# Moving the add of two expert results from VectorE to GpSimd at the end of a two-layer perceiver kernel

## The chip, the core and the metric

The kernel runs on one core of one Trainium2 chip. The metric is the device time of one execution in microseconds (us). Before the change the median of three runs is 888.03 us (887.79 to 888.46).

## What is computed

The reference runs two layers over `x`, 64 sequences of 32 rows of 256 values, 2048 rows in all, in float32. Only the last of six blocks matters here, a mixture of experts with two chosen experts per row and one shared expert:

```python
router_probs = softmax(flat @ router_w + router_b)
topk_probs, topk_idx = top_k(router_probs, 2)
weights = zeros_like(router_probs).at[arange(T)[:, None], topk_idx].add(topk_probs)
shared_out = gelu(flat @ sw1 + sb1) @ sw2 + sb2
h1 = gelu(einsum('td,edh->teh', flat, rw1) + rb1)
expert_out = einsum('teh,ehd->ted', h1, rw2) + rb2
mixed = einsum('ted,te->td', expert_out, weights)
x = x + shared_out + mixed
```

So each row of the output is x, plus the shared expert's row, plus two expert rows, each times its own weight.

## The kernel before

The 2048 rows are 4 groups (`NG`) of 4 tiles (`NT`) of 128 rows. `xs[g]` holds group g in SBUF as 128 partitions x 4 tiles x 256 values. The tiles of rows that go to experts are gathered, multiplied and written to a buffer in HBM, `r_rows`, by indirect DMAs that GpSimd issues (`outputs`, from L1948, issue at L1964). `r_rows` has one row for each pair of a row of x and one of its two choices.

When the last of these writes has landed, the end of the kernel begins, L2015 to L2064, and this is where the change is:

- **Loads** (L2020 to L2022). For each group and each choice (`which` is 0 or 1) SyncE issues one DMA of 512 KB from `r_rows` into `r[g][which]`, which has the shape of `xs[g]`: eight loads, in the order (0,0), (0,1), (1,0) and so on to (3,1).
- **Weights on ScalarE** (`weigh`, L2033). ScalarE multiplies tiles of `r` by the rows' weights, in place, one activation for each tile of 128x256. `by_scalar` (L2028) says which: in groups 0, 1 and 2 the tiles 2 and 3 of choice 0 and all four of choice 1; in group 3 all four of choice 0 and none of choice 1.
- **Sums on VectorE** (`sum_up`, L2039). For each choice and each pair of tiles: where ScalarE has weighted them, one `tensor_tensor` of 128x512 adds the pair to x; where not, two `scalar_tensor_tensor` of 128x256 multiply by the weight and add to x. So group 0, 1 or 2 takes two fused instructions (choice 0, tiles 0 and 1), then three adds of a pair (choice 0, tiles 2 and 3; choice 1, tiles 0 and 1; choice 1, tiles 2 and 3). Group 3 takes two adds and four fused instructions. Behind each pair of choice 1, SyncE issues a DMA of 256 KB from x to the output (L2053), eight in all.
- **Shared expert.** `fill_outputs` puts four matmuls for each tile on TensorE, into PSUM, and `settle` lets VectorE add the two tiles of such a bank to x (`x<-ps_so,x`, 128x512). Four of these pairs are left for the end. The first is settled ahead of `sum_up(0)`, the others one by one between the groups (L2058 to L2064). They use two banks in turn.

Every engine takes its instructions in the order in which the program names them (the switch at L511 keeps that order). So VectorE's order at the end is: settle, group 0, settle, group 1, settle, group 2, settle, group 3. ScalarE's order is the tiles of group 0, choice 0 before choice 1, then group 1 and so on. GpSimd has nothing to do after its last indirect write. Nothing that one engine does waits for another except where they touch the same part of a tile; such waits are semaphores that the framework puts in. The helper at L107 records nearly every operation, so in the profile lines are told apart by tiles: `x<-r,w,x` is the fused instruction, `x<-x,r` the add of a pair, `x<-ps_so,x` the settle, `r<-r,w` ScalarE's weighting.

Of the kernel before, what the change touches and what calls it, by code (L numbers as in the profile page):

```python
# [12 lines left out]
ALU = mybir.AluOpType  # L13
# [7 lines left out]
NG, NT = 4, 4  # L21
# [44 lines left out]
def perceiver_kernel(ctx: ExitStack, tc: tile.TileContext, a: dict, out: bass.AP):  # L66
# [32 lines left out]
    class InOrder:  # L99
# [12 lines left out]
    vector, scalar, gpsimd, sync = (  # L112
        InOrder(e) for e in (nc.vector, nc.scalar, nc.gpsimd, nc.sync)
    )
# [974 lines left out]
    def settle(n=None):  # L1089
        for _ in range(len(owed) if n is None else n):  # L1090
            owed.pop(0)()
# [529 lines left out]
    def mixture():  # L1621
# [395 lines left out]
        r = [(whole[:, 0], whole[:, 1]), (whole[:, 2], whole[:, 3])]  # L2017
# [6 lines left out]
        def weight(g, which, t):  # L2024
            at = which * nt + g * NT + t
            return pw[:, at : at + 1]

        def by_scalar(g, which):  # L2028
            if g == NG - 1 and which == 1:
                return ()  # L2030
            return range(NT) if which or g == NG - 1 else range(2, NT)

        def weigh(g):  # L2033
            for which in range(2):
                for t in by_scalar(g, which):
                    rows_t = r[g][which][:, t, :]
                    scalar.activation(rows_t, rows_t, AF.Copy, scale=weight(g, which, t))

        def sum_up(g):  # L2039
            for which in range(2):  # L2040
                for t0 in range(0, NT, 2):
                    if t0 in by_scalar(g, which):
                        x = xs[g][:, t0 : t0 + 2, :]
                        vector.tensor_tensor(x, x, r[g][which][:, t0 : t0 + 2, :], ALU.add)
                    else:
                        for t in range(t0, t0 + 2):
                            x = xs[g][:, t, :]
                            vector.scalar_tensor_tensor(
                                x, r[g][which][:, t, :], weight(g, which, t), x, ALU.mult, ALU.add
                            )  # L2050
                    if which == 1:
                        sync.dma_start(
                            out=out_view[g][:, t0 : t0 + 2], in_=xs[g][:, t0 : t0 + 2]  # L2053
                        )

        for g in range(NG):
            weigh(g)
        fill_outputs(2)  # L2058
        settle()
        sum_up(0)  # L2060
        for g in range(1, NG):
            fill_outputs(2)
            settle()
            sum_up(g)  # L2064

    out_view = out.rearrange("(g t p) d -> g p t d", g=NG, p=P)
    mixture()
    attention.close()

# [151 lines left out]
```

## Time and profile before

| what | value |
|---|---|
| median of three runs | 888.03 us |
| the profiled execution, its own time | 888.15 us |
| its span, first to last instruction | 886.4 us |
| granted TensorE clock, mean of the span | 0.992 |
| TensorE busy | 851.0 us (96%) |
| VectorE busy | 576.1 us (65%) |
| ScalarE busy | 438.5 us (49%) |
| GpSimd busy | 513.9 us (58%) |

The shares are means over the whole program. The part that the change touches is the last 21 us of the span, from 865.4 us on, when TensorE has only the shared expert left. In the views, DVE is VectorE, ACT is ScalarE, POOL is GpSimd, PE is TensorE and SP is SyncE; an operation is written out<-in by the names of tiles. A row of the timeline has the start and the length in us, merges neighbours of one kind (`x3` is three instructions), and shows in brackets the idle time ahead of it and who ended it. Two instructions of one engine overlap a little in the records, so the spacing of their starts is shorter than one's length.

### The profile page before, as it was taken

To read this page: it belongs to the slowest core of one execution; us is meant where nothing else is said; L and a number is where in the kernel's file an instruction comes from. 1 tells how busy PE (TensorE), PEld (TensorE's weight loads), DVE (VectorE), ACT (ScalarE), POOL (GpSimd) and SP (SyncE) were. 2 spreads that over 40 slices of the span, in tenths; PEclk is the share of its full clock that TensorE was granted. 3 is DMA by queue.
4 is the path that set the end of the run, shared out by engine and by line. 5 is a ranking of instruction groups with operands and counts; after the bars stand their busy time and mean duration, and the time that the engine had idled before them with its cause. 6 is when DMAs were issued, how large, how long until landed. Compare 5 with 4: busy or idle time off the path is not lost. (4 is left out here: it accounts for less than half of the span.)

```text
span 886.4 us, 22890 instructions
## 1 busy us (share of the span) xinstructions
PE 851.0 (96%) x8729; PEld 586.9 (66%) x8729; DVE 576.1 (65%) x1692; ACT 438.5 (49%) x1135; POOL 513.9 (58%) x1004
## 2 busy tenths in 40 slices
PE   7989999999999999999999999999999999999995
PEld 3566666665466666666666665666667568888894
DVE  6888777896777576885778756866766861111116
ACT  2756667674654555565445645575652323222224
POOL 4677777785774657575575754685651254555430
PEclk9999999999999999999999999999999999999999
DMA  6564433553110111110111101120010046777768
GB/s 216 146 164 119 120 92 96 143 138 104 54 55 24 34 54 55 55 55 2 55 54 56 55 1 55 55 73 25 3 36 2 24 169 219 232 232 232 220 191 290
DMA packets 66926, 88.77 MB, mean 100 GB/s; under 512 B 32480, under 2 KB 50688, under 8 KB 64768
## 3 DMA queue, kind: packets, MB, share of 16 engines
q1 hardware_dynamic: 62592, 76.95, 28.9%
q0 software_dynamic: 3456, 9.44, 3.2%
q8 instruction: 69, 1.13, 0.5%
q10 hardware_dynamic: 768, 0.92, 0.4%
q14 instruction: 41, 0.34, 0.1%
HBM read 65.78 MB, written 13.11 MB: 89 GB/s over the span
## 5 line engine op out<-in xcount | busy, mean ns | idle before, releaser
L107 ACT ACTIVATE e<-e,xnm 128x257 f32<-128x257 f32 x256 | 127.2, 499 | 43.7 <-DVE xnm L107 40.4
L119 PE MATMUL ps_k<-ct,w_w_l1x 128*128 128x512 f32 x256 | 122.8, 602 | 1.1 <-ACT yT L107 0.5
L107 POOL TENSOR_SCALAR e<-e,xsm 128x256 f32<-128x256 f32 x256 | 123.4, 500 | 0.0
L107 DVE CUSTOM_DVE_ANT_0 e<-ps_s,mask 128x257 f32<-128x257 f32 x256 | 93.5, 421 | 43.3 <-PE ps_s L119 43.1
L119 PE MATMUL ps_v<-w_w_l1x,ct 128*128 128x256 f32 x512 | 121.1, 379 | 0.0
L122 PE MATMUL ps_t<-cst,e 128*128 128x128 f32 x640 | 101.7, 281 | 2.3 <-DVE eT L107 2.0
L119 PEld LDWEIGHTS ps_v<-w_w_l1x,ct 128*128 128x128 f32 x512 | 93.4, 190 | 10.8 <-ACT y L107 0.2
L107 DVE COPY eT<-ps_t 128x512 f32<-128x512 f32 x124 | 85.1, 686 | 23.4 <-PE ps_t L122 23.3
L107 ACT ACTIVATE kT<-ps_k,vec 128x512 f32<-128x512 f32 x64 | 44.0, 687 | 97.9 <-PE ps_k L119 96.4
L107 POOL TENSOR_TENSOR x<-x,rows 128x256 f32<-128x256 f32 x96 | 70.0, 747 | 28.2 <-DVE y L107 24.9
L107 ACT ACTIVATE hTr<-ps_h,w 128x256 f32<-128x256 f32 (+1 forms) x80 | 31.4, 450 | 110.3 <-issue 89.4
L122 PEld LDWEIGHTS ps_t<-cst,e 128*128 128x128 f32 x640 | 71.4, 140 | 20.1 <-DVE eT L107 4.8
L107 DVE TENSOR_TENSOR og<-ps_o,b 128x512 f32<-128x512 f32 (+1 forms) x20 | 12.8, 638 | 105.6 <-PE ps_o L119 105.6
L119 PEld LDWEIGHTS ps_k<-ct,w_w_l1x 128*128 128x128 f32 x256 | 44.6, 190 | 42.0 <-issue 34.1
L1964 POOL DMA_INDIRECT r_rows<-og,lv x36 | 35.5, 986 | 60.8 <-DVE og L107 55.9
L119 PE MATMUL ps_h<-ygT,w 128*128 128x256 f32 (+1 forms) x320 | 67.2, 364 | 0.0
L107 ACT COPY v<-ps_v 128x512 f32<-128x512 f32 x80 | 46.4, 581 | 41.1 <-PE ps_v L119 40.7
L107 POOL TENSOR_TENSOR last<-e,xsm 128x4 f32<-128x4 f32 x64 | 15.3, 238 | 88.6 <-DVE xsm L107 87.1
L119 PE MATMUL ps_o<-w,hTr 128*128 128x256 f32 x288 | 65.3, 379 | 0.0
L119 PEld LDWEIGHTS ps_h<-ygT,w 128*128 128x128 f32 x320 | 56.0, 194 | 6.4 <-issue 0.2
L119 PEld LDWEIGHTS ps_o<-w,hTr 128*128 128x128 f32 x288 | 54.4, 190 | 7.2
L107 ACT ACTIVATE kb<-kT,cst 128x256 f32<-128x256 f32 x96 | 45.4, 512 | 23.8 <-POOL kT L107 23.7
(225 smaller groups left out, 1671.4 us busy)
## 6 DMA issues: line engine op xcount, KB each, us to landing
ct<-in_ctxT SPq DMA_DIRECT2D x16, 1024.0 KB
w<-in_ew SPq DMA_DIRECT2D x20, 514.0 KB
w<-in_ew SPq DMA_DIRECT2D x20, 512.0 KB
far<-part SPq DMA_DIRECT2D x126, 64.0 KB
v_rows<-v SPq DMA_DIRECT2D x16, 256.0 KB
vb<-v_rows SPq DMA_DIRECT2D x64, 64.0 KB
r<-r_rows SPq DMA_DIRECT2D x8, 512.0 KB
b<-in_eb SPq DMA_DIRECT2D x20, 128.0 KB
```

The source lines that it names most:

```text
L107: ins = getattr(self.engine, name)(*args, **kw)
L119: return kept(nc.tensor.matmul(ps, **args))
L122: return kept(nc.tensor.transpose(ps, src, eye))
L1964: wrote = nc.gpsimd.indirect_dma_start(out=r_rows, out_offset=bass.IndirectOffsetOnAxis(ap=write_i[:, at : at + 1], axis=0), in_=o[:, i, : ...
```

## The change

For groups 0, 1 and 2, GpSimd adds the weighted tiles 2 and 3 of choice 0 to the weighted tiles 2 and 3 of choice 1, in place in `r[g][1]`, with one `tensor_tensor` of 128x512. VectorE no longer adds that pair of choice 0 to x; the pair of choice 1, which now holds the sum of both, is added as before. Group 3 is as it was. In GpSimd's order the three adds come after all its indirect writes.

```diff
+        def added(g):
+            pair = r[g][0][:, 2:NT, :]
+            if g < NG - 1:
+                gpsimd.tensor_tensor(r[g][1][:, 2:NT, :], r[g][1][:, 2:NT, :], pair, ALU.add)
+
         def weigh(g):
...
         def sum_up(g):
             for which in range(2):
                 for t0 in range(0, NT, 2):
+                    if which == 0 and t0 == 2 and g < NG - 1:
+                        continue
                     if t0 in by_scalar(g, which):
...
         for g in range(NG):
             weigh(g)
+            added(g)
         fill_outputs(2)
```

## The prediction

> **What bounds the end now.** I read first the chain of work that ended last, in order of time:
>
> ```profile
> 877.56 1.06 DVE x L107 x3
> ...
> 879.08 1.34 DVE x L107 x3
> 880.42 0.09 issue
> ...
> 880.88 1.08 DVE x L107 x2
> ...
> 882.36 0.79 DVE x L107 x2
> ```
>
> It is VectorE alone, up to its last add into x. Then the timeline, VectorE alone and ScalarE alone:
>
> ```profile
> 871.88 1.49 DVE L107 TENSOR_TENSOR x<-x,r 128x512 f32<-128x512 f32 x2 [0.82 <-ACT r L107]
> 873.29 0.68 DVE L107 TENSOR_TENSOR x<-ps_so,x 128x512 f32<-128x512 f32 x1
> ...
> 877.88 1.89 DVE L107 TENSOR_TENSOR x<-x,r 128x512 f32<-128x512 f32 x3
> 879.68 0.68 DVE L107 TENSOR_TENSOR x<-ps_so,x 128x512 f32<-128x512 f32 x1
> 880.28 1.28 DVE L107 TENSOR_TENSOR x<-x,r 128x512 f32<-128x512 f32 x2
> 881.49 1.67 DVE L107 SCALAR_TENSOR_TENSOR x<-r,w,x 128x256 f32<-128x256 f32 x4
> ```
>
> ```profile
> 870.95 2.50 ACT L107 ACTIVATE r<-r,w 128x256 f32<-128x256 f32 x6 [0.60 <-DMA r<-r_rows]
> 873.89 2.51 ACT L107 ACTIVATE r<-r,w 128x256 f32<-128x256 f32 x6 [0.44 <-DMA r<-r_rows]
> 876.70 3.38 ACT L107 ACTIVATE r<-r,w 128x256 f32<-128x256 f32 x8 [0.30 <-DMA r<-r_rows]
> ```
>
> From 871.88 on VectorE shows no more idle time in brackets, to 883.15. ScalarE is paced by the loads; single rows of a narrower window give the ends of its tiles of groups 0, 1 and 2: 872.65, 875.60 and 878.41. VectorE runs close behind. It starts the last add of group 2 at 879.08, only 0.67 us after ScalarE's end. That margin decides this change. The loads' semaphores show the rest of the DMA side: (3,1) lands at 879.78, then six 256 KB outputs that had queued behind the loads land about 0.66 us apart (880.42 to 883.72), and the last two at 884.55 and 885.32, each about 2.15 us after its issue (882.39, 883.18).
>
> **What the change removes.** Three VectorE adds `x<-x,r` of 128x512. One lasts 0.684 us, but starts follow 0.60 us apart, so 3 x 0.60 = 1.8 us. Only about 0.26 us of it could reach the end: eight outputs at 0.66 us behind the last load give 879.78 + 8 x 0.66 = 885.06, against 885.32 now.
>
> **What it adds.** Three GpSimd adds of two SBUF inputs, 128x512. The row of groups has this form for another tile:
>
> ```profile
> L107 POOL TENSOR_TENSOR kT<-near,far 128x512 f32<-128x512 f32 x16 | 20.3, 1272 | 15.7 <-DMA far<-part 11.1 <-ACT kb L107 2.2 <-ACT yT L107 2.0
> ```
>
> I take 1.27 us (all 61 of this form: 1.262 least, 1.504 most). `near<-near,cst` starts 0.08 us after the ScalarE instruction it waited for; VectorE starts 0.035 us after GpSimd. So a new wait stands ahead of VectorE's last add of each group, and behind it in VectorE's queue stand the settle and the whole next group; SyncE's outputs wait for those. Without any disturbance the result of group g is there 0.08 + 1.27 + 0.035 = 1.39 us after ScalarE's end, but VectorE came 0.67 us after that end in group 2.
>
> **Shared reading.** A second cost appears where both engines read two SBUF inputs at once. The timeline at 190 us:
>
> ```profile
> 190.39 1.50 POOL L107 TENSOR_TENSOR qT<-near,far 128x512 f32<-128x512 f32 x1 [0.37 <-DMA far<-part]
> ...
> 191.21 1.23 DVE L107 TENSOR_TENSOR y<-y,big 128x512 f32<-128x512 f32 x1
> ...
> 191.86 1.18 POOL L107 TENSOR_TENSOR x<-x,rows 128x256 f32<-128x256 f32 x1
> ...
> 192.48 1.10 DVE L107 TENSOR_TENSOR q<-y,big 128x512 bf16<-128x512 f32 x1
> ```
>
> VectorE's add of two SBUF inputs takes 1.23 us instead of some 0.66 and ends 0.55 us after GpSimd's end (191.89); GpSimd's next takes 1.18 instead of 0.73 and ends 0.60 after VectorE's. They go by turns, and the one that waits ends about 0.13 us less than its own length after the other. The fused form suffers too: `conv<-yT,vec,conv` 128x248 takes 0.477 us alone and up to 0.83 beside GpSimd. An add with one input in PSUM doesn't: `x<-ps_p,x` takes 0.36 to 0.42 us with GpSimd beside it and without. So the settles stay free, while `x<-r,w,x` and `x<-x,r` queue with GpSimd.
>
> [...] With no 0.13 us back at each hand-over the sum below would be 2.26 us instead of 1.94; the rows above decide for the smaller.
>
> **The sum**, by starts in us of the profiled execution (spacing 0.60 for a pair, 0.39 for a fused one):
>
> - Group 0: GpSimd 872.65 + 0.08 = 872.73 to 874.00. VectorE ends its add of tiles 0 and 1 at 872.58, as before, then stands until 874.04. Settle 874.64. TensorE's last pair waits for that bank: it now starts some 1.3 us later than 874.03 and ends near 879.1, still ahead of its settle.
> - Group 1: fused 875.24 and 875.64. GpSimd asks at 875.68, behind the second fused one (ends 876.12): done 876.12 + 1.27 - 0.13 = 877.26. The add of tiles 0 and 1, asked for at 876.03, ends 877.26 + 0.55 = 877.81; the last add starts 877.73, settle 878.33.
> - Group 2: GpSimd 878.41 + 0.08 = 878.49 to 879.76. The first fused one, asked for at 878.93, ends 879.76 + 0.48 - 0.13 = 880.11; the next starts 880.03, the add of tiles 0 and 1 880.42, the last add 881.02.
>
> Before, that last one started at 879.08: **+1.94 us**. All behind it (settle, two adds, four fused, the last output, the closing) is the same queue at the same spacing, its loads long landed, and the last two outputs find the DMA queue empty, so it moves as a whole: span 886.40 + 1.94 = 888.34, own time 888.15 + 1.94 = 890.09. The profiled run stands 0.12 above the median, so 888.03 + 1.94 = 889.97; I say **890.0 us**.
>
> **Unknown: GpSimd's first arithmetic after indirect DMAs.** The trace has none. The nearest row is the turn the other way: the first indirect DMA after arithmetic started 0.84 us after its wait was over, later ones 0.28, and took 1.28 instead of 0.98, so (0.84 - 0.28) + 0.30 = 0.86 us extra. The low end is 0: nothing in GpSimd's row suggests a gain. With 0.86, group 0 ends at 874.86; GpSimd's second add then gets in first, and the same steps give a last add at 881.29, +2.2 us. I take 0, since the 9 us of idle time before may hide it, and keep +2.2 for the range. With all three adds as long as the longest row (1.50) as well, the steps give 881.75, +2.7, and the runs shown stand up to 0.43 above their median: 891.2 at the top.
>
> **Rivals.**
> 1. *No contention on these tiles.* Then only the new wait counts: the last add of group 2 starts at 878.49 + 1.27 + 0.035 = 879.80, **+0.71**, 888.7 us. For it: `near<-near,cst` on GpSimd keeps 1.27 us beside VectorE. Against: the rows at 190 us have exactly two SBUF inputs on each side.
> 2. *Not slower.* GpSimd's adds are done before VectorE needs them; then the shorter queue counts, and the outputs allow 0.26 us: 887.8. It decides from an add under 0.56 us (879.08 - 878.49 - 0.035); the shortest row is 1.262.
> 3. *GpSimd starts late.* The closing DRAIN on GpSimd, after the last indirect write ended at 863.83, ends only at 869.79, 5.96 us later; the other engines' DRAINs end about 0.05 us after their last instruction. If GpSimd pays this when its next arithmetic arrives, the first add ends near 879.97; the alternation then puts the last add of group 2 near 886.8, **+7.7**, 895.7. Against: the 5.96 us may pass while it is idle, long before 872.7.
>
> [...]
>
> **How the numbers follow.** Forecast 62%, its own range 889.4 to 891.2; rival 1 with part-way cases (888.6 to 889.4) 24%; rival 3 10%; rival 2 4%. The range 888.6 to 891.2 leaves out rivals 2 and 3, 14%. A change under 0.2% (1.78 us, bounds 886.25 and 889.81) can't be told from none. +1.94 lies just over it: of the forecast's 62% I put 46 above and 16 below. Slower 0.46 + 0.10 + 0.02 = 0.58; faster 0.02; within 0.40.
>
> **What would show it.** Right: VectorE idle about 1.4 us ahead of group 0's last add, put down to POOL; GpSimd rows of 1.3 to 1.6 us; the first `x<-r,w,x` of group 2 stretched to over 1 us; 4 us of new VectorE time and idle against 1.8 removed. Rival 1: all rows 0.48 and 0.68. Rival 3: GpSimd's first add starting near 878.7. Wrong altogether: VectorE's last add of group 2 at or ahead of 879.1.

## The result, and the profile after

The changed kernel is slower, by little. Its median is 889.74 us (888.37 to 893.68, 19 runs) against 887.79 us (885.67 to 890.44, 19 runs) of the kernel before in the same rounds; the ratio is 1.0026, with an interval of 1.0017 to 1.0035, so 1.5 to 3.1 us. The forecast was 890.0 us. The profiled execution took 890.36 us, with a span of 888.6 us.

The chain that ended last, after the change:

```profile
878.78 1.81 DVE x L107 x2
880.59 0.09 issue
880.68 0.13 DVE x L107
```

It is still VectorE, but a piece of two instructions now takes 1.81 us: one of them is held up. The timeline of VectorE alone shows where the rest went (start, length, and in brackets the idle time ahead and who ended it):

```profile
873.37 0.69 DVE L107 TENSOR_TENSOR x<-x,r 128x512 f32<-128x512 f32 x1 [1.45 <-POOL r L107]
...
877.49 0.69 DVE L107 TENSOR_TENSOR x<-x,r 128x512 f32<-128x512 f32 x1 [1.26 <-POOL r L107]
878.10 0.68 DVE L107 TENSOR_TENSOR x<-ps_so,x 128x512 f32<-128x512 f32 x1
878.70 1.89 DVE L107 SCALAR_TENSOR_TENSOR x<-r,w,x 128x256 f32<-128x256 f32 x2
880.68 1.29 DVE L107 TENSOR_TENSOR x<-x,r 128x512 f32<-128x512 f32 x2
```

and GpSimd's:

```profile
872.07 1.26 POOL L107 TENSOR_TENSOR r<-r 128x512 f32<-128x512 f32 x1 [8.89 <-ACT r L107]
876.19 1.26 POOL L107 TENSOR_TENSOR r<-r 128x512 f32<-128x512 f32 x1 [2.86 <-ACT r L107]
878.91 1.40 POOL L107 TENSOR_TENSOR r<-r 128x512 f32<-128x512 f32 x1 [1.46 <-ACT r L107]
```

A wait for another engine's result shows as idle time in the brackets; an instruction that is held up after its start shows as a longer row. In groups 0 and 1 VectorE stands idle for GpSimd (1.45 and 1.26 us). In group 2 it does not stand idle: its two fused instructions take 1.89 us instead of 0.87, because one of them lies beside GpSimd's third add. Three adds fewer, worth 1.8 us, don't make up for that.

Profiles of two executions also differ ahead of the change: this one reached its end stage 0.65 us earlier. So I compare **the stretch** from the landing of the last indirect write (865.27 us before, 864.62 after) to the end of the span. A landing is the last of the 16 completion events that the trace has for each transfer (those of the last write came from 865.11 to 865.27 us before); they are read from the trace's semaphore events. The stretch is 21.1 us before and 24.0 us after. The difference of 2.9 us is more than the forecast's 1.94, and one thing in it need not be the change's: in this profile the loads from (1,0) on landed some 1 us later after the last write ((2,1) at 12.4 us instead of 11.35), held up by the last 3 of each load's 16 events, the first of them 0.56 to 0.76 us behind the 13th. When GpSimd's first add began, 7.45 us after the last write, those 3 of (1,0) were still out, where before all 16 were in at 7.10. That each event is one DMA engine's, as the expectation of the second profile has it, is a reading; the trace names no engine. The same kernel in a second profile, below, has its loads on time and a stretch of 23.1 us.

### The profile page after: what moved, and what is told of

Read it like the earlier page. It is cut to its first block, busy times and chain, and to the rows that moved or that the text cites. A ratio compares the mean times of both kernels' runs of the same rounds, so it can differ in the third digit from the quotient of the medians.

```text
span 888.6 us, 22890 instructions
## 1 busy us (share of the span) xinstructions
PE 851.4 (96%) x8729; PEld 587.2 (66%) x8729; DVE 576.2 (65%) x1689; ACT 438.5 (49%) x1135; POOL 516.8 (58%) x1007
## 5 line engine op out<-in xcount | busy, mean ns | idle before, releaser
L107 DVE TENSOR_TENSOR og<-ps_o,b 128x512 f32<-128x512 f32 (+1 forms) x20 | 12.8, 638 | 105.6 <-PE ps_o L119 105.6
```

Of the source, the lines that this page charges most:

```text
L107: ins = getattr(self.engine, name)(*args, **kw)
```

## The experiments

The theory was the forecast's: a new wait, and turns on reading. The rivals were the wait alone, any work on GpSimd, and late loads that the change itself causes. All numbers "after the last write" count from its landing.

| kernel | load (2,1) lands, us after the last write | stretch, us | time against before, ratio with interval |
|---|---|---|---|
| before | 11.35 | 21.1 | |
| before, again | 12.32 | 21.6 | |
| changed | 12.42 | 24.0 | 1.0026 (1.0017 to 1.0035) |
| changed, again | 11.31 | 23.1 | 1.0022 (1.0006 to 1.0037) |
| adds beside, nobody waits | 11.84 | 22.9 | 1.0019 (1.0003 to 1.0035) |
| three memsets for each add | 11.33 | 22.4 | 1.0015 (1.0000 to 1.0031) |
| two memsets for each add | 12.71 | 23.0 | 1.0010 (0.9989 to 1.0031) |
| group 0 alone | 11.32 | 22.4 | 1.0009 (0.9989 to 1.0028) |
| group 2 alone | 11.88 | 22.4 | 1.0002 (0.9985 to 1.0020) |
| the waiting add put off | 12.28 | 22.5 | 1.0004 (0.9985 to 1.0024) |
| one tiny GpSimd add at the very end | 11.32 | 25.0 | 1.0053 (1.0032 to 1.0074) |

Timed runs of one kernel scatter by several us, so the ratios in the middle of the table decide little; the verdicts rest on the stretches and rows, of one profile for each line of the table.

**Both kernels again.** No edit.

> The changed kernel once more. In its profile the loads from (1,0) on landed 1.1 us later after the last indirect write than in the profile of before, held up by 3 of the 16 DMA engines before GpSimd's first add began. If that is chance (theory), the loads' landings go back to 7.1, 8.6, 10.1, 11.4, 13.1 and 14.5 us after the last write and the stretch from that write to the end is 21.07 + 1.9 = 23.0 us. If the change delays the loads (rival), they are at 8.2, 9.8, 11.1, 12.4, 13.9 and 15.3 again and the stretch is 23.9 us.

> The kernel before once more, for a second profile of its end. If late loads are chance, they can appear here too; the stretch from the last indirect write's landing to the end is 21.1 us where the loads land as in the first profile, and up to 0.5 us more where they land 1.1 us later (ScalarE then holds up the last add of group 2). If the change delays the loads, this profile has landings within 0.2 us of the first.

The loads were on time in the changed kernel (7.1, 8.6, 10.0, 11.3, 12.8 and 14.2 us) and late in the kernel before ((2,1) at 12.3). Over all eleven profiles, one to three of a load's 16 completion events fall behind by 0.7 to 1.7 us somewhere in the loads in six. One of the six is the kernel before, where GpSimd has nothing to do; another is "group 2 alone", where (1,0) landed late, at 7.63 us, and GpSimd's only add began at 13.76. So late loads need no GpSimd add. What brings them about stays open, and eleven profiles can't say whether GpSimd's adds make them more frequent. With loads on time the change costs 23.1 - 21.1 = 2.0 us, against the forecast's 1.94. With late loads it costs 24.0 - 21.6 = 2.4 us, by one pair of profiles that isn't quite like with like: in the kernel before only the loads from (2,1) on were late. VectorE and GpSimd of the changed kernel, again:

```profile
875.81 0.87 DVE L107 SCALAR_TENSOR_TENSOR x<-r,w,x 128x256 f32<-128x256 f32 x2
876.77 2.19 DVE L107 TENSOR_TENSOR x<-x,r 128x512 f32<-128x512 f32 x2
878.88 0.68 DVE L107 TENSOR_TENSOR x<-ps_so,x 128x512 f32<-128x512 f32 x1
879.48 1.64 DVE L107 SCALAR_TENSOR_TENSOR x<-r,w,x 128x256 f32<-128x256 f32 x2
```

```profile
876.38 1.43 POOL L107 TENSOR_TENSOR r<-r 128x512 f32<-128x512 f32 x1 [1.82 <-ACT r L107]
879.17 1.27 POOL L107 TENSOR_TENSOR r<-r 128x512 f32<-128x512 f32 x1 [1.36 <-ACT r L107]
```

This is the forecast's course step by step. GpSimd's second add waits for a fused instruction (1.43 us); VectorE's pair of adds waits for it (2.19 instead of 1.29); the settle between, with one input in PSUM, keeps 0.68; the first fused one of group 2 waits for the third add (1.64 instead of 0.87).

**Reading without waiting.** The kernel before, with GpSimd's adds beside it:

```diff
+        aside = sb.tile([P, 2, D], F32, tag=wide[4], name="aside")
+
+        def added(g):
+            pair = r[g][0][:, 2:NT, :]
+            if g < NG - 1:
+                gpsimd.tensor_tensor(aside, r[g][1][:, 2:NT, :], pair, ALU.add)
+
         def weigh(g):
...
         for g in range(NG):
             weigh(g)
+            added(g)
         fill_outputs(2)
```

> The kernel before, with the three GpSimd adds of 128x512 put beside it: they read the same weighted tiles at the same points, but write to a tile that nobody reads, so VectorE keeps all its adds and waits for none of them. Theory (turns: an instruction with two SBUF inputs on VectorE and one on GpSimd run one after the other): first GpSimd add 872.73 to 874.5, VectorE's fused pair of group 1 and its adds pushed, the last add of group 2 at 881.6 instead of 879.08 in the time of the execution before, so about +2.5 us, with single VectorE rows of over 1 us. Rival (wait alone): no VectorE row longer than 0.69 us and +0 us.

```profile
876.46 1.29 DVE L107 SCALAR_TENSOR_TENSOR x<-r,w,x 128x256 f32<-128x256 f32 x2
...
880.08 1.29 DVE L107 SCALAR_TENSOR_TENSOR x<-r,w,x 128x256 f32<-128x256 f32 x2
881.29 2.96 DVE L107 TENSOR_TENSOR x<-x,r 128x512 f32<-128x512 f32 x3
```

```profile
875.31 1.76 POOL L107 TENSOR_TENSOR aside<-r 128x512 f32<-128x512 f32 x1 [8.77 <-ACT r L107]
878.95 1.74 POOL L107 TENSOR_TENSOR aside<-r 128x512 f32<-128x512 f32 x1 [1.88 <-ACT r L107]
881.75 1.35 POOL L107 TENSOR_TENSOR aside<-r 128x512 f32<-128x512 f32 x1 [1.06 <-ACT r L107]
```

Nobody waits for these adds, and still VectorE's rows lengthen by 0.42, 0.42 and 1.07 us (1.29 for 0.87 twice, 2.96 for 1.89), and GpSimd's own by up to 0.5. The stretch is 22.9 us. The wait alone would have given 21.1, or up to 21.6 by late loads. The price is lower than the 2.5 us expected, 1.8: the second add came 0.5 us later with its loads, fell partly beside a settle, and cost 0.4 us. So rival 1, the wait alone, falls: contention is real, and its size hangs on what VectorE is doing when GpSimd begins.

**Waiting without reading.** GpSimd's add gives way to memsets, which read nothing; three of 512, 256 and 512 columns, then two of 512:

```diff
-                gpsimd.tensor_tensor(r[g][1][:, 2:NT, :], r[g][1][:, 2:NT, :], pair, ALU.add)
+                gpsimd.memset(r[g][1][:, 2:NT, :], 0.0)
+                gpsimd.memset(r[g][1][:, 3:NT, :], 0.0)
+                gpsimd.memset(r[g][1][:, 2:NT, :], 0.0)
```

> The changed kernel with each GpSimd add replaced by three memsets (512, 256 and 512 columns) over the pair that VectorE waits for, some 1.3 us together. They write and read nothing. It leaves out the experts' rows of tiles 2 and 3 of groups 0 to 2 (zeros are added). The wait stays as long, but GpSimd doesn't read. Theory (turns come from reading on both sides): only the wait is left, VectorE's last add of group 2 starts 1.4 us after ScalarE's last tile of group 2 (0.67 before, 2.46 after the change), +0.7 us on the kernel before, no stretched VectorE rows. Rival (any GpSimd work holds VectorE up): VectorE rows stretched as after the change and +1.9 us.

> As the run with memsets in place of the adds, with two of 512 columns instead of three (1.1 us instead of 1.48). It leaves out the experts' rows of tiles 2 and 3 of groups 0 to 2. Theory: only the wait counts, last add of group 2 1.2 us after ScalarE's end of group 2 and 14.3 us after the last write (13.8 before), VectorE rows all under 0.70 us, stretch 21.6 to 21.9 (TensorE's last pair may come late once more and cost up to 0.3). Rival (any GpSimd work holds VectorE up): rows over 0.8 us and a stretch of 22.5 or more.

With two memsets VectorE and GpSimd in group 2 look like this:

```profile
879.48 0.87 DVE L107 SCALAR_TENSOR_TENSOR x<-r,w,x 128x256 f32<-128x256 f32 x2
880.44 1.29 DVE L107 TENSOR_TENSOR x<-x,r 128x512 f32<-128x512 f32 x2
```

```profile
879.88 1.10 POOL L107 MEMSET r<- 128x512 f32 x2 [1.64 <-DMA out<-x]
```

They overlap, and VectorE's rows have their usual lengths. No VectorE row at the end of either kernel is longer than 0.70 us. So it isn't any work on GpSimd that brings the turns: the add that reads two SBUF inputs did (1.29 us for VectorE's fused pair, above), the memset that only writes did not (0.87).

The sizes missed. The three memsets took 1.48 us together, not 1.3, and VectorE stood idle for 0.45 us ahead of an add of group 1, which the profile puts down to nothing that it shows (the kernel with two memsets has the same 0.45 us there, the kernels with adds have not; what it was stays open). So its last add of group 2 started 1.71 us after ScalarE's end, not 1.4, and TensorE's last pair ended late (below), for 0.28 us more: +1.3 instead of +0.7. With two memsets the last add of group 2 started 1.23 us after ScalarE's end, as expected, but its loads were 1.4 us late, so VectorE would have started some 0.03 us after that end without the wait (an estimate from the kernel before with late loads, where it was 0.03), and by it the wait cost 1.2 us instead of 0.5.

**One group at a time.** `g < NG - 1` becomes `g == 0`, or `g == 2`, in both places.

> The change for group 0 alone: one GpSimd add, and VectorE skips one add. VectorE has nothing else to do while GpSimd adds, so nothing can block; the wait stands alone. VectorE's last add of group 0 starts 1.39 us after ScalarE's last tile of group 0 instead of 0.03, and all behind it moves by 1.35 us: last add of group 2 at 15.2 us after the last indirect write instead of 13.8 (loads on time), stretch to the end 22.4 us instead of 21.1, no VectorE row over 0.70 us. If ScalarE's and the loads' pace held the later groups up anyway (rival), the 1.35 us are made good by group 2 and the stretch is 21.1 to 21.5.

> The change for group 2 alone. VectorE's last add of group 2 starts 1.39 us after ScalarE's last tile of group 2 instead of 0.67, so +0.7 us: stretch 21.8 us with loads on time. VectorE reaches the wait before GpSimd begins, so no row is stretched. If the turns on reading were a fixed price of each GpSimd add (rival), +1.2 us and a stretched VectorE row.

Group 0 alone, VectorE:

```profile
876.45 0.69 DVE L107 TENSOR_TENSOR x<-x,r 128x512 f32<-128x512 f32 x1 [1.46 <-POOL r L107]
```

Every other row keeps its length. The last add of group 2 starts 15.14 us after the last write instead of 13.81, and the stretch is 22.4 us, +1.33 against the 1.35 expected. Nothing behind it makes the loss good: VectorE has no idle time left from there to the end. Group 2 alone, VectorE's last add of group 2:

```profile
880.56 0.69 DVE L107 TENSOR_TENSOR x<-x,r 128x512 f32<-128x512 f32 x1 [1.30 <-POOL r L107]
```

It starts 1.38 us after ScalarE's end, 1.39 expected, and no row is stretched. The stretch is 22.4 us with loads 0.5 us late; 0.54 us less by ScalarE's end gives 21.8, the number expected. So the wait's price is as the forecast had it, and a GpSimd add cost no turn here where VectorE had nothing to read (1.26 us for the add, 0.69 for VectorE's on either side of it).

**Hiding the wait.** VectorE's last add of a group comes behind the next group's first work:

```diff
...
         def sum_up(g):
...
+            sum_pair(g, 0, 0)
+            sum_pair(g, 0, 2)
+            if g > 0:
+                sum_pair(g - 1, 1, 2)
+            sum_pair(g, 1, 0)
+            if g == NG - 1:
+                sum_pair(g, 1, 2)
```

> The change with VectorE's last add of each of groups 0 to 2 put off behind the next group's first work (settle, fused pair or first adds), so that the wait is hidden. What is left is 1.8 us saved and the turns. Theory (turns cost): VectorE's fused instructions or adds beside a GpSimd add stretch to over 0.8 us, its first fused instruction of group 3 starts at 16.4 us after the last indirect write (16.2 before), stretch 21.1 to 21.4. Rival (wait alone): that instruction starts near 15.0, VectorE no longer bounds, and the outputs behind the loads end the kernel 0.26 us earlier, 20.8.

```profile
872.41 1.28 DVE L107 SCALAR_TENSOR_TENSOR x<-r,w,x 128x256 f32<-128x256 f32 x2 [0.22 <-DMA r<-r_rows]
...
876.05 1.58 DVE L107 SCALAR_TENSOR_TENSOR x<-r,w,x 128x256 f32<-128x256 f32 x2
...
879.36 2.36 DVE L107 TENSOR_TENSOR x<-x,r 128x512 f32<-128x512 f32 x3
```

No VectorE row waits for POOL any more, but GpSimd's adds stretch three rows instead: a fused one takes 0.88, another 1.18, an add 1.15 us. Group 3's first fused instruction starts at 17.3 us. Loads were late; beside the kernel before with late loads (16.6 us, stretch 21.6) the stretch of 22.5 is 0.9 longer. Hiding the wait doesn't save the change: of the 1.8 us that VectorE is spared, 1.6 come back as turns (0.41, 0.70 and 0.47), and with these late loads it also stands idle 0.22 us for a load and 0.54 for ScalarE. No kernel here beat the kernel before, and by the forecast's estimate the outputs behind the loads would have allowed a gain of only about 0.26 us.

**GpSimd's closing DRAIN.** In every profile it ended 5.96 to 5.98 us after GpSimd's last instruction.

```diff
             sum_up(g)
+        aside = sb.tile([P, 2], F32, tag=wide[4], name="aside")
+        gpsimd.tensor_tensor(aside, xs[NG - 1][:, NT - 1, 0:2], xs[NG - 1][:, NT - 1, 0:2], ALU.add)
```

> The kernel before, with one tiny GpSimd add (128x2, into a tile that nobody reads) behind VectorE's last instruction. In every profile so far the closing DRAIN on GpSimd ends 5.96 to 5.98 us after GpSimd's last instruction, whether that was an indirect DMA, an add or a memset. If it is a fixed price paid after GpSimd's last instruction, the DRAIN ends near 18.2 + 6.0 = 24.2 us after the last indirect write, behind the last output (20.1), and the stretch to the end is 24.9 us instead of 21.1: +3.8 us. If it passes while the engine waits (rival), +0.3 us at most.

GpSimd's row, and the closing line's group, whose columns are the least, median and longest length in ns and the first and last start in us:

```profile
883.50 0.20 POOL L107 TENSOR_TENSOR aside<-x 128x2 f32<-128x2 f32 x1 [19.42 <-issue]
```

```profile
L2219 POOLq DRAIN  x3: 45/113/6206, 883.5 to 890.2; - x3
```

The first DRAIN starts with the tiny add and ends 6.2 us later, at 889.7, long after the last output (20.0 us after the last write, so 885.5). The stretch is 25.0 us, +3.9, and the timed ratio 1.0053 (1.0032 to 1.0074). An instruction of 0.2 us costs nearly 4 us because it stands last on GpSimd.

## Why the prediction was right, point by point

- **The bound** (VectorE, close behind ScalarE): right, as before and after show.
- **1.8 us removed:** nearly right. The sum took 0.39 us from the second fused instruction of a group to the next add. Where the pair of choice 0 is taken away, that add works on the tiles that the fused ones have just written; it then starts 0.09 us after their end instead of 0.08 ahead of it, and the spacing is 0.56 to 0.57 us (0.40 in the groups that keep all adds, in "group 2 alone" too). This reason for it is read from the program's order, not tested. That little of the 1.8 us could reach the end was not seen by itself, since it never became free.
- **The wait, 1.39 us after ScalarE's end:** measured 1.38 us in group 2 alone, and +1.33 instead of 1.35 in group 0 alone.
- **The turns:** right in place, and nearly in size. In the second profile of the changed kernel the ones that waited ended 0.13, 0.14 and 0.19 us less than their own length after the other (0.13 in the sum). The last add of group 2 started at 15.83 us after the last write; the forecast's 881.02 is 15.75. That the two lie within 0.1 us is partly luck: up to group 2's first fused instruction VectorE ran 0.1 to 0.2 us ahead of the sum, and the longer spacing above took it back.
- **The first add after indirect DMAs**, taken at 0: right, though the trace of before couldn't settle it. It started 0.08 us after ScalarE's tile and took 1.26 us.
- **Rival 3 read the closing DRAIN wrongly.** It took the 5.96 us for something that GpSimd might owe after indirect DMAs. The runs show that the DRAIN ends 5.96 to 5.98 us after GpSimd's last instruction, be it an indirect DMA, an add or a memset.
- **TensorE's last pair:** the forecast had it end near 879.1 by its usual 3.7 us. It took 5.4 us in both profiles of the changed kernel and ended 15.4 to 15.5 us after the last write (the forecast's 879.1 is 13.8), still ahead of its settle.
- **The tail of the queue** moved as a whole with loads on time. What the forecast left out is that late loads can raise the price (2.4 us against 2.0, by one pair of profiles): in the kernel before with late loads VectorE's last add of group 2 started 0.03 us after ScalarE's end instead of 0.67, so there is no margin in which the wait can hide.

## What to carry to other kernels

Before work goes from a busy engine to an idle one, compare the moment at which the busy one needs the result with the moment at which the idle one can have it: here VectorE came 0.67 us after ScalarE, and with GpSimd's sum it could start only 1.38 us after it (group 2 alone). Then look for rows in the trace where both engines read two SBUF inputs at once; if they stretch (here to 1.89 us for 0.87), the second engine is no help while the first one reads. An engine that closes with a long DRAIN (5.96 us here) should get its last work early: a last add of 0.2 us on GpSimd cost 3.9 us.

## What else the runs showed of the hardware

**GpSimd's closing DRAIN** takes 5.96 to 5.98 us after its last instruction, where ScalarE's and VectorE's end 0.03 to 0.05 us after theirs. In the run with the waiting add put off it already mattered: GpSimd's third add ended late, its DRAIN ended at 21.64 us after the last write, SyncE's last at 21.39, and the end came some 0.27 us later for it.

**TensorE's clock.** The change leaves TensorE idle longer ahead of its last pair (2.88 us instead of 1.55). The stage of that pair (start and end, length, busy us and instructions of PE, PEld, DVE, ACT and POOL, then the granted clock, the DMA share and GB/s):

```profile
874.80:880.00 5.20, 5.20 (x16) 4.05 (x16) 3.85 (x7) 4.98 (x14) 2.35 (x2) 0.67 1.08 375
```

Before, it was 1.00 in that stage. The granted clock was 0.5 for 3.41 us in the records, and matmuls took 0.63 instead of 0.38 us. Over the kernels here, idle times of 2.75, 2.88, 2.89 and 3.07 us had this; one of 3.02 us had not, nor had those of 1.55 us and less. So the length of the idle time alone does not decide it, and what does is not shown.
